# Routers, their norms and the expert tables moved on behind every second piece of other work; gates from a hyperbolic tangent

## The chip, the cores and the metric

The kernel runs on one core of one Trainium2 chip. The metric is the device time of one execution in microseconds (us). A core has five engines with a queue of instructions each, which run in order: TensorE (PE in the profile, its weight loads PEld), VectorE (DVE), ScalarE (ACT), GpSimd (POOL) and SyncE (SP). SP, ACT and POOL also issue DMA transfers. An instruction that waits for a semaphore holds up what stands behind it on its engine.

## What is computed

Sixty-four sequences of 64 tokens with 128 features pass four layers; a second tensor of the same shape is the context. Layer 0 is attention with relative positions and a feed-forward part. Layer 1 is self-attention, cross-attention and a feed-forward part. Layer 2 gates pooled context into the tokens. Layer 3 is self-attention, cross-attention and a mixture of eight experts, of which each token takes two. The change touches that mixture:

```python
h = _ln(x, ln_g, ln_b)
logits = h @ rw.T + rb
vals, idx = jax.lax.top_k(logits, K)          # K = 2
gates = jax.nn.softmax(vals, axis=-1)
...
h1 = jax.nn.gelu(jnp.einsum('nd,efd->enf', hf, fc1_w) + fc1_b[:, None, :], approximate=False)
eo = jnp.einsum('enf,edf->end', h1, fc2_w) + fc2_b[:, None, :]
...
mixed = (gathered * gates_f[..., None]).sum(axis=1).reshape(x.shape)
return x + mixed
```

Of two logits a >= b the softmax gives 1/(1+e) and e/(1+e) with e = exp(b - a), which is the same as 0.5 + 0.5 tanh((a - b)/2) and 0.5 - 0.5 tanh((a - b)/2).

## The kernel before

The 4096 tokens are cut into eight groups (g = 0 to 7) of 512 tokens, four blocks of 128. Layer 0 runs first, in an order written out by hand. Everything after it is written as Python generators, which issue a piece of their instructions and then yield. A driver, `drive` (line 149), decides whose piece is issued next. Outside layer 0 the order in which instructions are issued here is a priority: a scheduler in the language lays each engine's final order, and may put an instruction ahead of earlier ones when it takes it to be ready.

The driver goes round in rounds. In each it may start one attention task (self-attention or cross-attention of one group) and one light task (feed-forward of layer 1, or layer 2). Attentions are started four rounds apart, three once no light task is left. Then each running task issues one piece, in the order of their start. Then the driver takes a step of the `fill` generator, which is `experts` (line 669): one step a round, and two or three by turns once the flag `done["exponentials"]` is set. When all tasks have ended, the rest of `fill` is issued at once.

`cross3` (line 1292) is the last attention of a group. It has 15 pieces before its closing one, which adds the result to `x`. Then, still in the same generator, come the norm (`normalise`, line 281, into the tile `zx`, four buffers), the transposes, and `router` (line 1320): the logits `lg`, the two best experts by comparisons (`cand`, `hot`), the difference `e2` and its exponential (called `e` in the profile), the rank of each token in its expert by two matmuls (`pr`), the gates, and eight scatters of rows, `hrows<-zx,to`, indirect DMAs that POOL issues. The column of `zx` that holds the token number is written by a copy from `tok`, which depends on nothing but the buffer. At the end the router counts up `done["routed"]`. In the last group three of the router's yields are left out.

The eight groups are in two parts, five and three (`PARTS`). `experts` waits until five groups are routed, makes the first table (`table`, line 677: which expert's rows lie in which slot of 128 rows), waits for the exponentials flag, which the last group's cross-attention sets when it issues its last softmax exponentials, and goes through 47 slots of the first part and 31 of the second. In each slot: a load of 128 rows on SP (`km<-hrows`, which waits until all scatters of its part have landed), a transpose (`xt`), an activation on ACT (`vp`), four matmuls with the first expert matrix and four with the second (all named `f`; the profile counts each twice, so sixteen per slot), Gelu on ACT, an addition on DVE, and a scatter on POOL (`yrows<-km,tob`). The second part's table waits until all eight groups are routed. At the end the rows are read back, weighted by the gates (`summed`, line 820), and written out.

Of the kernel before, what the change touches and what calls it, by code (L numbers as in the profile page):

```python
# [12 lines left out]
AF = mybir.ActivationFunctionType  # L13
ALU = mybir.AluOpType
AX = mybir.AxisListType

P = 128
# [5 lines left out]
NBLK = T // P  # L23
# [10 lines left out]
ROWW = D + 2  # L34
# [60 lines left out]
def kernel(ctx: ExitStack, tc: tile.TileContext, a: dict, out: bass.AP):  # L95
    order = {"on": False}
    nc = Ordered(tc, order)
# [14 lines left out]
    def wtile(shape, tag, bufs, dtype=F32):  # L112
        if tag in COMMON:
            return pools["common"].tile(shape, dtype, tag=tag, bufs=COMMON[tag], name=tag)
        return pools["work"].tile(shape, dtype, tag=tag, bufs=bufs, name=tag)
# [29 lines left out]
    def mid(ap, n):  # L145

        return ap.unsqueeze(1).to_broadcast([ap.shape[0], n, ap.shape[1]])

    def drive(phases, lags, ends, fill):

        todo = {kind: [] for kind in lags}
        for n, (start, kind) in enumerate(phases):
            for g in range(NG):
                todo[kind].append((n, g, start))

        todo["light"].sort(key=lambda task: task[1])
        passed = {(-1, g) for g in range(NG)} - {(-1, g) for g, gen in ends}
        count = 0
        running, wait = [(-1, g, gen) for g, gen in ends], {kind: 0 for kind in lags}
        while running or any(todo.values()):
            for kind, tasks in todo.items():
                if wait[kind] <= 0:
                    for task in tasks:
                        n, g, start = task
                        if (n - 1, g) in passed:  # L170
                            tasks.remove(task)
                            running.append((n, g, start(g)))
                            wait[kind] = lags[kind] - (kind == "attention" and not todo["light"])
                            break
                wait[kind] -= 1
            for task in list(running):
                n, g, gen = task
                if next(gen, "end") == "end":
                    running.remove(task)
                    passed.add((n, g))  # L180
            count += 1
            for _ in range(2 + count % 2 if done["exponentials"] else 1):
                next(fill, "end")
        for _ in fill:
            pass

# [482 lines left out]
    def experts():  # L669
# [7 lines left out]
        def table(h):  # L677

            cnt = wtile([P, NE], "cnt", 1)
            nc.vector.tensor_tensor(cnt, endbase[h], start, ALU.subtract)  # L680
            cmp = v3(wtile([P, 512], "pT", 7)[:, 0 : NE * (REGION - 1)], NE)
            nc.vector.tensor_tensor(
                cmp, last(cnt[:, :], REGION - 1), mid(limit[:, :], NE), ALU.is_gt
            )
            nb = wtile([P, NE], "nb", 1)
            nc.vector.tensor_reduce(nb, cmp, axis=AX.X, op=ALU.add)
            cum = wtile([P, NE], "cum", 1)
            nc.vector.tensor_copy(cum[:, 0:1], nb[:, 0:1])
            for e in range(1, NE):
                nc.vector.tensor_tensor(cum[:, e : e + 1], cum[:, e - 1 : e], nb[:, e : e + 1], ALU.add)  # L690
            yield
            ns = NSLOT[h]
            counts = wtile([P, 512], "pT", 7)
            past = v3(counts[:, 0 : ns * NE], ns)
            jb, rb = (counts[:, (NE + k) * ns : (NE + k + 1) * ns] for k in range(2))
            nc.vector.tensor_tensor(past, last(index[:, 0:ns], NE), mid(cum[:, :], ns), ALU.is_ge)
            eb = wtile([P, ns], f"eb{h}", 1)
            nc.vector.tensor_reduce(eb, past, axis=AX.X, op=ALU.add)
            nc.vector.tensor_tensor(past, past, mid(nb[:, :], ns), ALU.mult)
            nc.vector.tensor_reduce(jb, past, axis=AX.X, op=ALU.add)  # L700
            yield
            nc.vector.tensor_tensor(jb, index[:, 0:ns], jb, ALU.subtract)
            nc.vector.scalar_tensor_tensor(rb, eb, float(REGION), jb, op0=ALU.mult, op1=ALU.add)

            nc.vector.tensor_scalar(rb, rb, float(NE * REGION), float(P), ALU.min, ALU.mult)
            tab = wtile([1, 2, ns], f"table{h}", 1, I32)
            nc.vector.tensor_copy(tab[:, 0, :], rb[0:1, :])
            nc.vector.tensor_scalar(
                tab[:, 1, :], eb[0:1, :], float(NE - 1), float(D), ALU.min, ALU.mult
            )  # L710

            hot = wtile([NE, ns], "hotb", 1)
            nc.vector.tensor_scalar(hot, eb[0:NE, :], lane[0:NE, :], None, ALU.is_equal)
            yield
            pb = extra("pb")
            for c in range(NFC):
                nc.tensor.matmul(
                    pb[:, c * ns : (c + 1) * ns], lhsT=fc1bT[:, c, :], rhs=hot, start=True, stop=True
                )
            hb = v3(wtile([P, NBLK * S], "mb", 3)[:, 0 : NFC * ns], NFC) if h == 0 else v3(room[:, used : used + NFC * ns], NFC)  # L720
            nc.vector.tensor_copy(hb, v3(pb[:, 0 : NFC * ns], NFC))
            tables[h] = tab, eb, hb
# [109 lines left out]

        while done["routed"] < PARTS[0]:
            yield
        yield from table(0)
        while not done["exponentials"]:
            yield

# [8 lines left out]
        for t in range(-6, total + 2):  # L847
            h = sum(t + 6 >= at for at in LAST)
            while h < NH and done["routed"] < sum(PARTS[: h + 1]):
                yield  # L850
            if h < NH and h not in tables:
                yield from table(h)
            if 0 <= t < total:
                first(t)
            if 0 <= t - 2 < total:
                second(t - 2)
            if t + 6 < total:
                load(t + 6)
            if 0 <= t + 1 < total:
                stage_weights(t + 1)  # L860
            if 0 <= t + 2 < total:
                turn(t + 2)

            for h in range(NH - 1):
                gl, at = divmod(t - 2 - LAST[h] - 4, 4)
                if 0 <= gl < PARTS[h]:
                    g = sum(PARTS[:h]) + gl
                    if at == 0:
                        reads[g] = read(g)
                    if at == 2:  # L870
                        summed(g, reads.pop(g))
            yield
# [8 lines left out]
    def other_layers(ends):  # L881
# [410 lines left out]
        def cross3(g):  # L1292
            x = xs[g]
            ct = ctx_of(g, 3)
            pc = transpose4(ct.rearrange("p b i -> p (b i)"))
            cz = wtile([P, T], "z", 4)
            nc.scalar.copy(cz, pc)
            yield
            kvT, qT = yield from together(
                ln_turned(cz, "ckv_g", "ckv_b", cz), ln_turned(x, "cq_g", "cq_b")  # L1300
            )
            add_row(x, obias[:, 1, :])
            yield
            ps = yield from attention(
                qT[:, :], v3(kvT[:, :], NB), in3[:, 1, 0:D], in3[:, 1, D : 2 * D], in3[:, 1, 2 * D :],
                wo3[:, 1, :], sc3, bias=1, then=(lambda: done.update(exponentials=True)) if g == NG - 1 else None,
            )
            nc.vector.tensor_tensor(x, ps, x, ALU.add)
            yield

            zx = wtile([P, NBLK, ROWW], "zx", 4)
            yield from normalise(zx.rearrange("p k c -> p (k c)"), x, width=ROWW)
            yield
            pt = transpose4(zx.rearrange("p k c -> p (k c)"), ROWW)
            hT = wtile([P, T], "T", 4)
            nc.scalar.activation(hT, pt, AF.Identity, scale=col("moe_g"), bias=col("moe_b"))
            yield
            yield from router(g, hT, x, zx)

        def router(g, hT, x, zx):  # L1320

# [7 lines left out]
            tops, hots = [], []  # L1329
# [22 lines left out]
            both = wtile([P, NBLK, NE], "both", 3)  # L1352
            nc.vector.tensor_tensor(both, hots[0], hots[1], ALU.add)
            e2 = wtile([P, NBLK], "e2", 3)
            g1 = wtile([P, NBLK], "g1", 3)
            nc.vector.tensor_tensor(e2, tops[1], tops[0], ALU.subtract)
            nc.scalar.activation(e2, e2, AF.Exp)
            yield

            pr = extra("pr")  # L1360
# [5 lines left out]
            for k in range(NBLK):  # L1366
                if k + 1 < NBLK:
                    dst = before[:, k + 1, :]
                else:
                    h, gl = PLACE[g]  # L1370
# [4 lines left out]
                )  # L1375
            nc.vector.tensor_tensor(before, before, v3(pr[:, 0 : NBLK * NE], NBLK), ALU.add)
            yield
            nc.vector.tensor_scalar(g1, e2, 1.0, None, ALU.add)
            nc.vector.reciprocal(g1, g1)
            nc.vector.tensor_copy(gate[:, g, 0, :], g1)  # L1380
            nc.vector.tensor_tensor(gate[:, g, 1, :], e2, g1, ALU.mult)

            def meta(c):
                return zx[:, :, D + c : D + c + 1].rearrange("p k c -> p (k c)")
# [48 lines left out]
    gate = mtile([P, NG, 2, NBLK], "gate")  # L1433
# [92 lines left out]
```

## Time and profile before

| what | value |
|---|---|
| three runs | 1685.83, 1694.06, 1694.51 us; median 1694.06 |
| the profiled execution | 1692.51 us, of it 1690.5 us from the first to the last instruction (the span) |
| busy share of the span | PE 92%, PEld 68%, DVE 69%, ACT 59%, POOL 53% |
| mean granted clock of PE | 0.943 |
| scatters of rows, `hrows<-zx,to` | 64, from 1415.8 to 1542.0 us |
| scatters of results, `yrows<-km,tob` | 78, mean 991 ns |
| ACT table loads | 2, mean 1283 ns |

Times of single instructions are counted from the start of the span. Almost all instructions carry line L74, the helper that records them, so they are told apart by engine, operation and tile: `a<-b,c` is an instruction that writes tile a and reads b and c. "Busy tenths" cut the span in 40 slices of 42.3 us, a digit being the busy share of an engine in tenths; PEclk is the share of full speed that was granted to TensorE's clock.

### The profile page before, as it was taken

To read this page: it belongs to the slowest core of one execution; us is meant where nothing else is said; L and a number is where in the kernel's file an instruction comes from. 1 tells how busy PE (TensorE), PEld (TensorE's weight loads), DVE (VectorE), ACT (ScalarE), POOL (GpSimd) and SP (SyncE) were. 2 spreads that over 40 slices of the span, in tenths; PEclk is the share of its full clock that TensorE was granted. 3 is DMA by queue.
4 is the path that set the end of the run, shared out by engine and by line. 5 is a ranking of instruction groups with operands and counts; after the bars stand their busy time and mean duration, and the time that the engine had idled before them with its cause. 6 is when DMAs were issued, how large, how long until landed. Compare 5 with 4: busy or idle time off the path is not lost. (4 is left out here: it accounts for less than half of the span.)

```text
span 1690.5 us, 45408 instructions
## 1 busy us (share of the span) xinstructions
PE 1548.2 (92%) x17588; PEld 1155.6 (68%) x17588; DVE 1161.5 (69%) x3147; ACT 1002.6 (59%) x2744; POOL 903.5 (53%) x867
## 2 busy tenths in 40 slices
PE   7799999999999999978888999989988998859995
PEld 4466666667666666646766776666767776759995
DVE  4477686777777677758887787677766677555554
ACT  4456556555555555535775655466767786427774
POOL 2445455555556464657886766653422234467543
PEclk9899999999999999979999999889998998759998
DMA  6756554555555555541000100000000000013243
GB/s 165 156 145 147 133 146 121 139 133 134 131 147 133 130 138 143 140 143 28 12 18 27 27 20 20 8 14 2 2 8 14 15 2 27 25 55 88 68 124 109
DMA packets 218356, 136.74 MB, mean 81 GB/s; under 512 B 38904, under 2 KB 202882, under 8 KB 218016
## 3 DMA queue, kind: packets, MB, share of 16 engines
q1 hardware_dynamic: 187024, 90.99, 23.1%
q10 hardware_dynamic: 26576, 34.40, 6.2%
q0 software_dynamic: 4544, 8.47, 1.6%
q8 instruction: 140, 2.29, 0.6%
q14 instruction: 72, 0.59, 0.1%
HBM read 66.95 MB, written 67.78 MB: 80 GB/s over the span
## 5 line engine op out<-in xcount | busy, mean ns | idle before, releaser
L74 ACT ACTIVATE s<-s,nm 128x128 f32<-128x128 f32 x512 | 198.1, 388 | 249.1 <-DVE nm L74 225.8
L74 POOL TENSOR_TENSOR s<-s,sm 128x512 f32<-128x512 f32 x128 | 130.4, 1039 | 251.8 <-DVE sm L74 251.8
L74 PE MATMUL pt<-ident,s 128*128 128x128 f32 x1536 | 216.3, 285 | 26.0 <-ACT kT L74 10.6
L74 POOL TENSOR_TENSOR s<-s,mx 128x512 f32<-128x512 f32 x160 | 164.3, 1046 | 99.1 <-DVE mx L74 92.9
L74 PEld LDWEIGHTS pt<-ident,s 128*128 128x128 f32 x1536 | 179.9, 146 | 46.4 <-issue 17.7
L74 ACT ACTIVATE pT<-pt 128x512 f32<-128x512 f32 x256 | 141.0, 601 | 78.1 <-PE pt L74 69.6
L74 POOL TENSOR_TENSOR skew<-skew,mb 128x512 f32<-128x512 f32 x128 | 159.9, 1271 | 40.3 <-DMA skew<-scr 39.6
L74 POOL TENSOR_TENSOR rs<-rs,nhalf 128x4 f32<-128x4 f32 x80 | 81.5, 1019 | 186.1 <-DVE rs L74 157.0
L74 PEld LDWEIGHTS av<-vb,pT 128*64 128x64 f32 x4096 | 134.1, 144 | 22.2 <-issue 13.2
L74 PE MATMUL av<-vb,pT 128*64 128x18 f32 x4096 | 142.3, 217 | 5.3 <-DVE o L74 4.8
L74 DVE TENSOR_REDUCE mx<-s 128x8 f32<-128x512 f32 x160 | 103.0, 677 | 44.4 <-ACT s L74 44.4
L74 PE MATMUL psk<-kv,wk 128*128 128x512 f32 x256 | 127.9, 622 | 0.0
L74 PE MATMUL psv<-wv,kv 128*128 128x256 f32 x512 | 127.4, 392 | 0.0
L74 PE MATMUL sc<-km,qs 32*64 32x256 f32 x2048 | 105.4, 422 | 9.4 <-ACT qs L74 5.4
L74 POOL DMA_INDIRECT yrows<-km,tob x78 | 77.3, 991 | 58.6 <-DVE tob L74 29.7
L74 DVE COPY pT<-pt 128x512 f32<-128x512 f32 x128 | 82.2, 683 | 37.3 <-PE pt L74 37.3
L74 PEld LDWEIGHTS pbd<-rT,qp 64*128 64x128 f32 x1024 | 63.0, 189 | 58.6 <-DVE qp L74 56.9
L74 PEld LDWEIGHTS psv<-wv,kv 128*128 128x128 f32 x512 | 92.2, 189 | 15.1 <-issue 1.0
L74 PEld LDWEIGHTS av<-pT,v 128*64 128x64 f32 x2048 | 66.5, 138 | 50.7 <-issue 29.0
L74 DVE TENSOR_TENSOR s<-sc,mb 128x512 f32<-128x512 f32 x128 | 82.5, 682 | 26.7 <-PE sc L74 26.7
L74 DVE TENSOR_TENSOR s<-psc,skew 128x512 f32<-128x512 f32 x128 | 87.5, 684 | 14.2 <-issue 6.3
L74 ACT ACTIVATION_READ_ACCUMULATOR s<-s,nm 128x1 f32 x512 | 95.6, 187 | 0.0
(231 smaller groups left out, 3564.0 us busy)
## 6 DMA issues: line engine op xcount, KB each, us to landing
scr<-stage SPq DMA_DIRECT2D x64, 516.0 KB
skew<-scr SPq DMA_DIRECT2D x128, 256.0 KB
hrows<-pad ACTq DMA_DIRECT2D x66, 325.0 KB
ctx<-in_ctxT SPq DMA_DIRECT2D x24, 256.0 KB
km<-hrows SPq DMA_DIRECT2D x78, 65.0 KB
fcw<-in_fc ACTq DMA_DIRECT2D x16, 256.0 KB
kv<-in_xT SPq DMA_DIRECT2D x8, 256.0 KB
kv<-in_ctxT SPq DMA_DIRECT2D x8, 256.0 KB
```

The source lines that it names most:

```text
L74: ins = it(*args, **kw)
```

## The change

The driver gets a second kind of task. A generator that yields the word `CHAIN` instead of nothing is noted as a chain, and from then on it isn't given one piece a round: it moves on after every second piece of the other tasks, once more at the end of the round, and after each step of the fill. The closing norm and the router of `cross3` become chains (with one yield more, after the tile `zx` is taken), and so does the making of a table in `experts`; while the fill is in a chain, its steps come with the chains. The gates are made from a hyperbolic tangent of half the difference of the two logits: the exponential, an addition, a reciprocal, a copy and a product become the tangent and two multiply-adds.

```diff
@@ -146,7 +146,14 @@
 
         return ap.unsqueeze(1).to_broadcast([ap.shape[0], n, ap.shape[1]])
 
+    CHAIN = "chain"
+
+    def chain(gen):
+        for _ in gen:
+            yield CHAIN
+
     def drive(phases, lags, ends, fill):
+
 
 
 
@@ -160,8 +167,25 @@
 
         todo["light"].sort(key=lambda task: task[1])
         passed = {(-1, g) for g in range(NG)} - {(-1, g) for g, gen in ends}
-        count = 0
+        count, chains, filling = 0, set(), [None]
         running, wait = [(-1, g, gen) for g, gen in ends], {kind: 0 for kind in lags}
+
+        def advance(task):
+            n, g, gen = task
+            said = next(gen, "end")
+            chains.discard(task)
+            if said == "end":
+                running.remove(task)
+                passed.add((n, g))
+            elif said == CHAIN:
+                chains.add(task)
+
+        def advance_chains():
+            for task in [task for task in running if task in chains]:
+                advance(task)
+            if filling[0] == CHAIN:
+                filling[0] = next(fill, "end")
+
         while running or any(todo.values()):
             for kind, tasks in todo.items():
                 if wait[kind] <= 0:
@@ -173,14 +197,19 @@
                             wait[kind] = lags[kind] - (kind == "attention" and not todo["light"])
                             break
                 wait[kind] -= 1
+            beats = 0
             for task in list(running):
-                n, g, gen = task
-                if next(gen, "end") == "end":
-                    running.remove(task)
-                    passed.add((n, g))
+                if task not in chains:
+                    advance(task)
+                    beats += 1
+                    if beats % 2 == 0:
+                        advance_chains()
+            advance_chains()
             count += 1
             for _ in range(2 + count % 2 if done["exponentials"] else 1):
-                next(fill, "end")
+                if filling[0] != CHAIN:
+                    filling[0] = next(fill, "end")
+                    advance_chains()
         for _ in fill:
             pass
 
@@ -832,7 +861,7 @@
 
         while done["routed"] < PARTS[0]:
             yield
-        yield from table(0)
+        yield from chain(table(0))
         while not done["exponentials"]:
             yield
 
@@ -849,7 +878,7 @@
             while h < NH and done["routed"] < sum(PARTS[: h + 1]):
                 yield
             if h < NH and h not in tables:
-                yield from table(h)
+                yield from chain(table(h))
             if 0 <= t < total:
                 first(t)
             if 0 <= t - 2 < total:
@@ -1309,13 +1338,14 @@
             yield
 
             zx = wtile([P, NBLK, ROWW], "zx", 4)
-            yield from normalise(zx.rearrange("p k c -> p (k c)"), x, width=ROWW)
-            yield
+            yield CHAIN
+            yield from chain(normalise(zx.rearrange("p k c -> p (k c)"), x, width=ROWW))
+            yield CHAIN
             pt = transpose4(zx.rearrange("p k c -> p (k c)"), ROWW)
             hT = wtile([P, T], "T", 4)
             nc.scalar.activation(hT, pt, AF.Identity, scale=col("moe_g"), bias=col("moe_b"))
-            yield
-            yield from router(g, hT, x, zx)
+            yield CHAIN
+            yield from chain(router(g, hT, x, zx))
 
         def router(g, hT, x, zx):
 
@@ -1352,9 +1382,8 @@
             both = wtile([P, NBLK, NE], "both", 3)
             nc.vector.tensor_tensor(both, hots[0], hots[1], ALU.add)
             e2 = wtile([P, NBLK], "e2", 3)
-            g1 = wtile([P, NBLK], "g1", 3)
-            nc.vector.tensor_tensor(e2, tops[1], tops[0], ALU.subtract)
-            nc.scalar.activation(e2, e2, AF.Exp)
+            nc.vector.tensor_tensor(e2, tops[0], tops[1], ALU.subtract)
+            nc.scalar.activation(e2, e2, AF.Tanh, scale=0.5)
             yield
 
             pr = extra("pr")
@@ -1375,10 +1404,9 @@
                 )
             nc.vector.tensor_tensor(before, before, v3(pr[:, 0 : NBLK * NE], NBLK), ALU.add)
             yield
-            nc.vector.tensor_scalar(g1, e2, 1.0, None, ALU.add)
-            nc.vector.reciprocal(g1, g1)
-            nc.vector.tensor_copy(gate[:, g, 0, :], g1)
-            nc.vector.tensor_tensor(gate[:, g, 1, :], e2, g1, ALU.mult)
+
+            nc.vector.tensor_scalar(gate[:, g, 0, :], e2, 0.5, 0.5, ALU.mult, ALU.add)
+            nc.vector.tensor_scalar(gate[:, g, 1, :], e2, -0.5, 0.5, ALU.mult, ALU.add)
 
             def meta(c):
                 return zx[:, :, D + c : D + c + 1].rearrange("p k c -> p (k c)")
```

## The prediction

> **What bounds it now.** First I read the busy tenths by slices: TensorE (PE) holds 9 in most slices and breaks once, to 8-8-5 in slices 34 to 36, some 1440 to 1520 us. That break is what I cost. I then cut the stretch into windows (start:end, us, then busy us of PE, PEld, DVE, ACT, POOL, granted clock, DMA share, GB/s):
>
> ```profile
> PE   7799999999999999978888999989988998859995
> PEclk9899999999999999979999999889998998759998
> ...
> 1400.00:1420.00 20.00, 19.29 (x271) 14.41 (x271) 16.99 (x77) 15.37 (x32) 7.78 (x8) 0.85 0.02 5
> 1450.00:1460.00 10.00, 4.94 (x42) 4.45 (x26) 5.75 (x25) 1.46 (x3) 2.56 (x3) 0.74 0.05 16
> 1490.00:1500.00 10.00, 1.83 (x9) 1.70 (x8) 2.23 (x19) 0.00 (x0) 7.82 (x9) 0.50 0.17 54
> 1500.00:1510.00 10.00, 6.13 (x24) 5.01 (x24) 7.26 (x55) 2.52 (x6) 7.68 (x8) 0.50 0.14 47
> 1560.00:1600.00 40.00, 40.00 (x358) 39.79 (x357) 20.68 (x93) 31.59 (x105) 21.51 (x22) 1.00 0.27 72
> ```
>
> PE is the limit up to 1420 and again from 1545, where the experts run. Between, it idles and its granted clock is 0.50, while POOL is the busiest engine. Weighting PE's busy time by the clock in ten-us windows leaves about 42 us of full-rate work in the 86 us from 1430 to 1516: some 44 us are to be had at most.
>
> The tile view of `zx` says what POOL does there, and the timelines of DVE and ACT who waits (start, duration; in brackets the idle time before and its releaser):
>
> ```profile
> L74 POOL DMA_INDIRECT hrows<-zx,to x64: 954/958/1274, 1415.8 to 1542.0; - x64
> L74 ACT ACTIVATE zx<-x,nmr,rs x32: 478/483/540, 1353.7 to 1501.4; 128x128 f32<-128x128 f32 x32
> ```
>
> ```profile
> 1430.23 0.17 DVE L74 COPY zx<-tok 128x4 f32<-128x4 f32 x1 [6.05 <-DMA hrows<-zx,to]
> ...
> 1453.27 0.17 DVE L74 COPY zx<-tok 128x4 f32<-128x4 f32 x1 [5.07 <-DMA hrows<-zx,to]
> ...
> 1500.02 0.16 DVE L74 SCALAR_TENSOR_TENSOR nmr<-mv,rs 128x4 f32<-128x4 f32 x1 [6.97 <-POOL rs L74]
> ```
>
> ```profile
> 1477.64 0.60 ACT L74 ACTIVATE pT<-pt 128x512 f32<-128x512 f32 x1 [0.26 <-PE pt L74]
> ...
> 1500.21 1.65 ACT L74 ACTIVATE zx<-x,nmr,rs 128x128 f32<-128x128 f32 x4 [11.94 <-DMA hrows<-zx,to]
> ...
> 1516.81 1.28 ACT L74 ACT_TABLE_LOAD   x1
> ```
>
> The first router's norm runs at 1353.7, its first scatter at 1415.8. All 64 row scatters come after that, each 0.96 us and 0.30 us to the next, 1.27 in all: 81 us of POOL, nearly back to back from 1486 to 1542. With four `zx` buffers, groups 4 and 5 wait for the scatters of groups 0 and 1, and group 7's norm 11.94 us for those of group 3. The experts need 40 of the scatters. The chain of waits shows them released by one of these, the load being followed by the first expert matmuls:
>
> ```profile
> 1510.36 2.27 DMA hrows<-zx,to
> ...
> 1513.87 1.91 DMA km<-hrows
> 1515.82 0.48 PE xt L74
> 1516.30 1.71 PE f L74 x8
> ```
>
> The last attention exponential had ended at 1478.2. So 38 us lie between it and the first expert, and they belong to late routers.
>
> **Why the routers are late.** From norm to logits, logits to `e`, and `e` to first scatter, group 0 takes 20 us each (1353.7, 1373.7, 1394.2, 1415.8): that is one start interval of cross3, three rounds of the driver. A router with norm has 12 pieces after its first and gets one a round. That is the order of issue, not data: group 7's norm-to-logits, with nothing else running, takes 5 us (1500.2 to 1505.2).
>
> **The change, part by part.** (1) *Driver.* Stepping through both loops piece by piece: with five other tasks running, chains advance after the second, the fourth, at the round's end and after the fill's step, four times a round. Group 0's router is issued in 3 rounds instead of 13; group 4's is done in round 123, table 0 in round 125, the round that issues the last attention exponentials. Before, these were rounds 132 and 133. The experts then start with that exponential. Nothing is added or removed; moved are, per router, some 30 small DVE operations of 0.15 to 0.19 us (about 5 us), 20 matmuls (`tr` 0.64, `pl` 1.06, `pr` 0.8: 2.5 us of PE at full clock), one ACT pass and 8 scatters (10.2 us of POOL).
>
> (2) *Where the scatters land.* Into the attention stretch, where POOL is busy about 6.4 us in 20 (`rs` three times 1.02, `s` twice 1.04, `x` 1.3). With 10.2 it is at 16.6 of 20: it fits, in bursts. What queues behind a burst on POOL is `rs` and `s`; DVE's `nmr` stands behind `rs`, and all DVE work behind `nmr`. Cost per burst: below, 0.9, the ordinary wait of `nmr` (no extra); above, the 6.97 of 1500.02, which came behind ten scatters. In the trace the two bursts that did run in the stretch (1415 to 1428, 1441 to 1452) brought no such wait, so I take no extra here and keep 6.97 for the range. On SP, the first expert load waits for the 40 scatters at the queue's head, and only later expert loads and the final transfers stand behind it: the last context load of an attention is issued with group 7's cross3 in round 113, ahead of it. 0.
>
> (3) *The zx copies.* The copy of the token numbers depends on the buffer alone and was placed on DVE before the scatters of four groups earlier had landed: 6.05 and 5.07 us on DVE, with 3.51 and 5.06 us of PE idle (its matmuls at 1433.16 and 1455.75). With early routers these two are gone (PE -8.6), but the same placement can recur behind each of the first four bursts: 0 to 4 times 4.3. Nearest are the two seen, one per burst; but the bursts now end long before the norms need the buffer, so I take two, +8.6.
>
> (4) *Router work moved forward.* The intervals grew 20.0, 20.6, 21.6 as routers joined; all are now like the last: +1.6 +1.0 = +2.6.
>
> (5) *Gates.* Out go `g<-e` 300 ns, reciprocal 170, copy 186, product 165; in come two operations like `zx<-ci` at 178: DVE -0.47 us a router, -3.7 in all. Only the final sums read the gates: 0 on the path, and 3.7 of DVE at most if that cover were gone.
>
> (6) *Tanh for Exp.* Same shape; `e<-e` took 209 ns, and on 128x512 Tanh took 630 against Exp 601: 0. The table is the open point. The trace has two table loads in all, one at the start and one before the first Gelu, so Tanh (used in the second layer) shares a set with Exp. Whether it shares Gelu's no row shows. Routers 6 and 7 now fall among Gelus: 0 to 4 loads of 1.28, 0 to 5.1 us. I take 0, since before every non-Gelu function among the experts (Identity on `vp`) needed no load; Exp kept there would run the same risk.
>
> The Trainium skill speaks against this part: "ScalarE: Activation LUTs", section "Table sets: the hidden batching unit", lists tanh with exp and with sigmoid and not with gelu, and asks to finish one set before the next; with its 2.66 us per switch, four switches would be an estimated 10.6 us. No run here shows which holds.
>
> **The sum**, on the profiled execution (span 1690.5, 1692.5 with its surroundings, so +2.0; 1.5 under the median 1694.06 of runs from 1685.83 to 1694.51). Last attention exponential 1478.2 - 8.6 + 8.6 + 2.6 = 1480.8, and there the first expert matmul. 78 slots of 1.90 (sixteen `f` 1.79, one `xt` 0.11, as the chain repeats them) = 148.2. PE work that now runs beside them: the last attention's end, some 3.5, and three routers, 7.5: 11. A start among scatters: before, PE waited 2.15 at 1541.4 and ran 1.85 slower after it: 4. From the last expert matmul to the end, as now, 1672.6 to 1690.5: 17.9. Together 1661.9, with 2.0 1663.9; +1.5 to the median: **1665 us**, 1.7% faster.
>
> **Rivals.** *The full gain.* No copy waits at all and no start among scatters: 1665 - 8.6 - 4 = 1652. For it: routers are two groups ahead of their buffers. Against: POOL serves 1.27 per expert slot and the last scatters still mix in.
> *POOL takes the place of the routers (the slower side).* Every burst from group 0 to group 6 falls on live attention and costs DVE the 6.97 us: 1665 + 7 x 6.97 = 1714. It outweighs the gain from (1694 - 1665) / 6.97 = 4.2 bursts. For it: POOL at 16.6 of 20, in order, with PE at 19.3 of 20 and nothing to catch up with. Against: the two bursts seen, though few `rs` fell near them.
> *The order of issue isn't what decides.* Instructions outside the first layer are reordered by a scheduler, as the copy at 733 us, long ahead of its router, shows; if the routers ran late for other reasons the time stays at 1694. Against: lags of exactly one interval per three pieces.
> *Tables.* Four loads: 1665 + 5.1 = 1670, the same side.
>
> **Numbers.** Chances: forecast, tables included, 0.47; full gain 0.23; POOL 0.20; no effect 0.10. About 0.5% (8.5 us) is what a measurement can tell from no change; the first two lie under 1685.6, so faster 0.70, same 0.10, slower 0.20. The range begins below the full gain by the four router periods' 2.6 and a further 8 for slots that slip in before the last exponential, 1641, and ends at 1700, with five bursts at full price. The forecast's own: none to four copy waits, with tables, 1656 to 1679.
>
> **What would show it.** Right: first scatter near 1375, the 40th by 1470; first `f` within 5 us of the last attention exponential; no slice under 8 before the end; ACT_TABLE_LOAD x2. Wrong: DVE waits for `rs` or for `hrows` of over 4 us in each interval after 1360 (step 2 or 3), loads beyond two (step 6), scatters still after 1415 (step 1).

## The result, and the profile after

The changed kernel takes 1707.28 us (median of four runs, 1705.94 to 1709.66) beside 1689.94 us of the kernel before in the same series (four runs, 1683.79 to 1694.51). The ratio is 1.010, 95% interval 1.008 to 1.012: **1% slower**, where 1.7% faster was forecast. 1707 lies above the range, which ended at 1700, and nearest to the rival in which POOL takes the place of the routers (1714).

The page of the changed kernel, in busy tenths, and the windows in the same stretches as before (us; busy us of PE, PEld, DVE, ACT, POOL; granted clock; DMA share; GB/s):

```profile
PE   7799999999999999969898999899989877878995
...
PEclk9899999999999999979999999889998978779998
```

```profile
1400.00:1420.00 20.00, 14.91 (x232) 11.36 (x218) 12.03 (x40) 12.83 (x25) 10.58 (x11) 0.93 0.07 25
1450.00:1460.00 10.00, 4.47 (x37) 3.54 (x38) 1.12 (x4) 2.43 (x5) 3.25 (x4) 0.50 0.06 20
1490.00:1500.00 10.00, 7.99 (x112) 6.91 (x112) 7.00 (x32) 5.75 (x12) 4.31 (x5) 0.96 0.06 16
1500.00:1510.00 10.00, 5.47 (x92) 5.24 (x92) 7.20 (x45) 2.53 (x6) 5.04 (x7) 0.89 0.13 40
```

The one break of 8-8-5 has become a long shallow one. From 1400 to 1420 us PE was busy 19.29 of 20 us before and is busy 14.91 now: the stretch that was full has holes. In 1450 to 1460 no engine is busy for even half the time: everybody waits. The tile view of `zx` and the timelines of POOL, DVE, ACT and PE (start, duration, in brackets the idle time before and its releaser) say for what:

```profile
L74 POOL DMA_INDIRECT hrows<-zx,to x64: 954/958/1232, 1377.2 to 1569.4; - x64
L74 ACT ACTIVATE zx<-x,nmr,rs x32: 477/482/495, 1352.1 to 1544.7; 128x128 f32<-128x128 f32 x32
```

```profile
1387.23 0.96 POOL L74 DMA_INDIRECT hrows<-zx,to  x1 [0.30 <-issue]
1388.22 1.05 POOL L74 TENSOR_TENSOR rs<-rs,nhalf 128x4 f32<-128x4 f32 x1
...
1389.31 0.16 DVE L74 SCALAR_TENSOR_TENSOR nmr<-mv,rs 128x4 f32<-128x4 f32 x1 [7.16 <-POOL rs L74]
...
1389.51 1.65 ACT L74 ACTIVATE zx<-x,nmr,rs 128x128 f32<-128x128 f32 x4 [6.74 <-DVE nmr L74]
...
1390.05 0.48 PE L74 MATMUL tr<-ident,zx 128*128 128x128 f32 x1 [6.62 <-ACT zx L74]
...
1421.61 0.16 DVE L74 SCALAR_TENSOR_TENSOR nmr<-mv,rs 128x4 f32<-128x4 f32 x1 [6.96 <-POOL rs L74]
...
1453.92 0.16 DVE L74 SCALAR_TENSOR_TENSOR nmr<-mv,rs 128x4 f32<-128x4 f32 x1 [6.96 <-POOL rs L74]
```

The first scatter comes at 1377.2 and not 1415.8 us, so routers did move forward. But the burst of group g ends exactly where the closing norm of group g+1 asks for its `rs`: on POOL `rs` starts 0.03 us after the last of eight scatters, DVE has by then waited 7.16 us, ACT 6.74 and PE 6.62. It happens to groups 1, 2 and 3 in the same way. In the next three norms DVE waits about 1 us for `rs`, and 4.82 in the last one (1543.3), when the experts already run.

At the other end, PE around the start of the experts, DVE's table, and ACT:

```profile
1508.93 0.23 DVE L74 TENSOR_SCALAR hotb<-eb,lane 8x47 f32<-8x47 f32 x1
...
1509.31 1.91 PE L74 MATMUL pb<-hotb,fc1bT 8*128 8x47 f32 x8 [4.53 <-DVE hotb L74]
1513.06 0.64 PE L74 MATMUL pr<-both,tri 128*128 128x32 f32 x2 [1.85 <-DVE mb L74]
...
1516.54 3.60 PE L74 MATMUL av<-vb,pT 128*64 128x18 f32 x64 [2.41 <-DVE before L74]
1520.07 0.48 PE L74 MATMUL xt<-ident,km 128*128 128x128 f32 x1
...
1522.27 1.87 PE L74 MATMUL pl<-rw,T 128*128 128x8 f32 x8 [0.66 <-ACT T L74]
1524.00 1.09 PE L74 MATMUL tr<-ident,o 128*128 128x128 f32 x4
1524.88 1.92 PE L74 MATMUL f<-vp,h 128*128 128x128 f32 x8
...
1525.72 1.28 ACT L74 ACT_TABLE_LOAD   x1
...
1531.62 0.19 ACT L74 ACTIVATE e<-e 128x4 f32<-128x4 f32 x1
```

The last attention exponential starts at 1507.1. Around and after it PE waits 4.53 + 1.85 + 2.41 = 8.8 us for the table (`hotb`, `mb`) and for a router (`before`), while the last attention's own products `av` stand behind them in its queue; the experts' first `xt` stands behind `av`, and the first `f` comes 17.7 us after the exponential. The tangent at 1531.62 lies between Gelus, and no table load follows it: two loads in all, as before.

Where the 15.5 us of span went (1690.5 before, 1706.0 after): first norm to last attention exponential, both by their starts, 124.0 -> 155.1 (+31.1); from there to the first `f` 38.5 -> 17.7 (-20.7, from unrounded times); from there to the end 174.4 -> 181.1 (+6.7); the stretch ahead -1.6.

### The profile page after: what moved, and what is told of

The parts are those of the page before. It is cut to its first block, busy times and chain, and to the rows that moved or that the text cites. A ratio compares the mean times of both kernels' runs of the same rounds, so it can differ in the third digit from the quotient of the medians.

```text
span 1706.0 us, 45367 instructions
## 1 busy us (share of the span) xinstructions
PE 1545.1 (91%) x17588; PEld 1154.5 (68%) x17588; DVE 1156.0 (68%) x3131; ACT 1002.6 (59%) x2744; POOL 903.2 (53%) x867
## 5 line engine op out<-in xcount | busy, mean ns | idle before, releaser
L74 PEld LDWEIGHTS av<-vb,pT 128*64 128x64 f32 x4096 | 138.2, 147 | 34.6 <-issue 18.0
L74 PE MATMUL av<-vb,pT 128*64 128x18 f32 x4096 | 146.7, 218 | 14.2 <-DVE o L74 9.1
L74 PEld LDWEIGHTS av<-pT,v 128*64 128x64 f32 x2048 | 66.5, 138 | 50.8 <-issue 29.1
L74 DVE TENSOR_TENSOR s<-sc,mb 128x512 f32<-128x512 f32 x128 | 82.4, 680 | 26.3 <-PE sc L74 26.3
```

Source lines behind the costliest of these rows:

```text
L74: ins = it(*args, **kw)
```

## The experiments

Theory **P**: the bursts of scatters hold up `rs` on POOL, and behind it DVE, ACT and PE. Rival **C**: four steps a round put a serial chain of small operations too close together, and the engines, which run in order, stand still at every link. Later, for the gap between the last exponential and the first `f`: **T**, the table's pieces on DVE and its products on PE hold up the end of the last attention, and **R**, the table's work tiles wait for buffers that the attentions use.

Kernels sent together ran on one chip with the kernel before, and ratios are to it. The kernels e5 to e8, and e17 and e18, ran in two sets in which the kernel before itself took 1726.6 us and engines waited in a way that no other set shows (the last section); their times stand only against the kernels of their own set. The table has the other sets.

| kernel | us | ratio [95%] | intervals of the zx norms, groups 0 to 4 | first norm to last exponential | to first `f` |
|---|---|---|---|---|---|
| before | 1689.9 | 1 | 20.0 20.6 21.6 25.1 | 124.0 | 38.5 |
| changed | 1707.3 | 1.010 [1.008, 1.012] | 37.4 32.3 32.3 19.3 | 155.1 | 17.7 |
| e1 rs by reciprocal on DVE | 1675.2 | 0.993 [0.991, 0.994] | 26.9 23.8 23.6 19.0 | 128.3 | 16.5 |
| e2 scatters one a step | 1685.4 | 0.998 [0.997, 1.000] | 30.7 27.5 27.2 18.5 | 135.3 | 21.8 |
| e3 before, tangent alone | 1684.2 | 0.998 [0.997, 0.999] | 20.0 20.6 21.0 26.3 | 124.7 | 34.5 |
| e4 before, copy tied | 1673.0 | 0.992 [0.990, 0.993] | 20.0 20.6 21.6 20.7 | 112.0 | 37.0 |
| e9 changed, again | 1711.1 | 1.011 [1.008, 1.014] | 37.5 32.3 32.4 19.2 | 156.8 | 17.7 |
| e10 rs by Newton on DVE | 1687.5 | 0.998 [0.997, 1.000] | 30.4 25.9 25.6 23.8 | 136.5 | 17.3 |
| e11 two steps a round | 1700.0 | 1.005 [1.003, 1.007] | 23.6 34.3 28.0 24.8 | 146.9 | 17.1 |
| e12 e10, other PSUM | 1695.9 | 1.002 [1.000, 1.004] | 30.1 29.1 26.9 25.0 | 146.0 | 17.4 |
| e13 e10, table in one piece | 1694.9 | 1.002 [1.000, 1.004] | 30.5 25.9 25.6 23.8 | 140.5 | 17.4 |
| e14 e10, two steps a round | 1688.8 | 0.998 [0.996, 1.000] | 23.6 26.5 26.3 23.1 | 136.7 | 19.6 |
| e15 late chains | 1697.9 | 1.003 [1.001, 1.005] | 21.1 23.6 45.1 20.2 | 147.2 | 16.6 |
| e16 e15 with Newton, table in one piece | 1683.9 | 0.995 [0.994, 0.997] | 20.8 22.8 34.7 23.7 | 136.4 | 17.7 |

### e1 and e2: rs away from the bursts, or the bursts cut up

e1, in `normalise` (it leaves out the square root, so it tells where the time goes and isn't a kernel to be had):

```diff
-        nc.gpsimd.tensor_tensor(rs, rs, nhalf, ALU.pow)
+        if width != D:
+            nc.vector.reciprocal(rs, rs)
+        else:
+            nc.gpsimd.tensor_tensor(rs, rs, nhalf, ALU.pow)
```

> The changed kernel, with DVE making the factor rs in the norm ahead of the router as a plain reciprocal of the variance, where POOL raised it to the power -0.5; so this norm divides by the variance instead of its root, and all other norms are left on POOL. Theory P (the bursts of eight scatters on POOL hold up rs, and behind it nmr on DVE, zx on ACT and the transposes on PE, some 6.6 us a burst beyond the usual wait, in four to six of the bursts): the 5 to 7 us waits of nmr for rs in the zx norms are gone, the intervals between zx norms fall from 32-37 to 22-30 us, time 1668 to 1685. Theory C (the finer steps put a serial chain of small operations between the others' pieces, and the engines, which run in order, stand still at each link; POOL only comes with it): the intervals stay at 30 us or more and the time at 1698 or above.

e2, in `router`, after each scatter:

```diff
+                    if g < NG - 1 and 2 * k + 1 + n < 2 * NBLK:
+                        yield
```

> The changed kernel with one scatter per step of the chain instead of eight in one step (groups 0 to 6). Theory P: what stands behind a burst on POOL is now at most one or two scatters late, so no wait of nmr for rs in the stretch is over 2.6 us, and the time is 1675 to 1695. Theory C: waits for rs shorten, but the intervals stay at 30 us or more and the time is 1700 or above.

e1: 1675.2 us, 32 us under the changed kernel (1707.3). DVE's waits from 1350 to 1500 us (total us, times, longest), first of the changed kernel, then of e1:

```profile
DVE nmr L74 <- POOL rs L74: 26.9, 9, 7.2
```

```profile
DVE rec L74 <- PE av L74: 19.1, 8, 5.1
...
DVE nmr L74 <- POOL rs L74: 2.1, 3, 0.8
```

And e1's timeline at a norm that falls on a burst:

```profile
1399.72 1.04 POOL L74 DMA_INDIRECT hrows<-zx,to  x1 [0.32 <-DVE mv L74]
1401.07 0.96 POOL L74 DMA_INDIRECT hrows<-zx,to  x1 [0.30 <-issue]
...
1399.96 0.18 DVE L74 RECIPROCAL rs<-rs 128x4 f32<-128x4 f32 x1
1400.17 0.16 DVE L74 SCALAR_TENSOR_TENSOR nmr<-mv,rs 128x4 f32<-128x4 f32 x1
```

The burst is still there; `nmr` follows `rs` in 0.21 us beside it. Nothing else was edited, and the stretch up to the last exponential shrinks by 26.7 us: P, not C, for this part. (What is left is still 16.3 us longer than in e4, below.) The three intervals shrink by 10.5, 8.5 and 8.7 us, 9.2 a burst: the 7 us that is read off the wait, and 2.2 more that the wait doesn't show. e2 gets there in part (longest wait for `rs` 3.6 us in place of 7.2, total 11.8; expected was 2.6 at most), 22 us under the changed kernel and within its expectation.

### e3 and e4: the parts alone, in the kernel before

e3 takes the gates of the change into the kernel before. e4 changes one instruction there:

```diff
-            nc.vector.tensor_copy(meta(0), tok[:, PLACE[g][1] * NBLK : (PLACE[g][1] + 1) * NBLK])
+            nc.vector.scalar_tensor_tensor(
+                meta(0), ci, 0.0, tok[:, PLACE[g][1] * NBLK : (PLACE[g][1] + 1) * NBLK],
+                op0=ALU.mult, op1=ALU.add,
+            )
```

> The kernel before with the gates from the hyperbolic tangent alone, driver untouched. Both theories: no effect beyond 0.3% (1685 to 1695), two table loads, since the tangent was followed by Gelu without a load in the changed kernel. If the tangent did cost table loads here, three or more loads and up to 5 us more.

> The kernel before, with the copy of the token numbers into zx made to depend on the router's own indices (their number times zero is added), so that it can't be laid ahead of its router. By step 3 of the prediction the two waits of DVE for hrows (6.05 and 5.07 us, 4.3 us of PE each) go, and the time falls by 8.6 us, to about 1681 to 1683; the wait of 11.94 us of group 7's zx stays. Rival: these waits only fill time in which the routers are late anyway, and the time stays within 3 us of before.

e3: 3.9 us less (0.23% of 1688.4; by the interval 1.9 to 5.7). In its profile the part between last exponential and first `f` is 4.0 shorter (38.5 -> 34.5), the stretch ahead 0.7 longer, the end 1.1 shorter; two table loads. e4: 15.5 us less, nearly twice the 8.6 expected. The windows of e4 and of the kernel before from 1420 to 1440 us:

```profile
1420.00:1440.00 20.00, 20.00 (x301) 16.47 (x300) 16.76 (x65) 13.07 (x25) 10.92 (x11) 0.91 0.17 51
```

```profile
1420.00:1440.00 20.00, 16.46 (x207) 12.72 (x205) 13.65 (x53) 11.16 (x19) 7.98 (x9) 0.90 0.15 52
```

With the copy tied to its router, PE has no idle time there, and the stretch falls by 11.9 us, more than the two waits of DVE that went (6.05 + 5.07 = 11.1). **e4 is faster than both kernels**, by one instruction, with the driver untouched.

e4 also says what early routers cost when no copy waits for scatters and no wait for `rs` in the stretch is over 1.2 us. Both hold for e1 as for e4, and the two ran beside each other; its stretch is 128.3 us against 112.0. Of the 16.3 us between them PE idles 11.2 (14.9 against 3.7) and is busy 5.1 longer, for the same attentions. No run takes these 16 us apart.

### e5 to e12: the same with all of the computation, half the rate, other PSUM buffers

Dividing by the variance, e1 may send tokens to other experts. e5 and e10 make the true factor on DVE:

```diff
-        nc.gpsimd.tensor_tensor(rs, rs, nhalf, ALU.pow)
+        if width != D:
+            var = rs
+            rs, sq = wtile([P, NBLK], "rt", 3), wtile([P, NBLK], "sq", 3)
+            nc.vector.tensor_scalar(
+                rs.bitcast(I32), var.bitcast(I32), -0.5, 1597463007.0, ALU.mult, ALU.add
+            )
+            for _ in range(3):
+                nc.vector.scalar_tensor_tensor(sq, rs, -0.5, rs, op0=ALU.mult, op1=ALU.mult)
+                nc.vector.tensor_tensor(sq, sq, var, ALU.mult)
+                nc.vector.scalar_tensor_tensor(rs, sq, 1.5, rs, op0=ALU.add, op1=ALU.mult)
+        else:
+            nc.gpsimd.tensor_tensor(rs, rs, nhalf, ALU.pow)
```

> The changed kernel with the factor rs of the norm ahead of the router made on DVE, by three steps of Newton from a first guess taken from the bits of the variance (eleven small DVE operations; all that the reference wants is computed). If e1 gained because rs no longer stands behind the scatters on POOL: 1672 to 1684, with intervals between zx norms of 23 to 28 us. If e1 gained because dividing by the variance sent tokens to other experts: near the changed kernel, 1700 or above.

> The changed kernel in which chains move on twice a round (at its end and after the fill's step) instead of four times; bursts of eight scatters as they are, rs on POOL. Theory P: the bursts still meet rs in most intervals, so waits of nmr for rs of 4 to 7 us stay, and the time is 1695 to 1710. Theory C (links of a serial chain too close together): the intervals fall to 22 to 27 us and the time to 1675 to 1690. Against both: the router takes 6 to 7 rounds instead of 3, so the experts may start up to 10 us later after the last attention exponential.

> The kernel of e5, with the router's rank products pr and the table's products pb in the seven rotating PSUM buffers instead of the single one that they share with the attention's products av. Theory T (pr and pb, which stand ahead of the last av and wait for DVE's table work, delay the end of the last attention): from the last attention exponential to the first expert f 8 to 12 us instead of about 17, time 5 to 9 us under e5. Rival: pb still stands ahead of av in PE's order and waits for hotb, so no more than 2 us.

> The kernel before (driver untouched) with everything else that has helped or may: the copy that can't be laid ahead (e4), tangent gates (e3), rs of the router's norm by Newton on DVE (e5), pr and pb in the rotating buffers. If the gains add up: 1688 - 15.5 - 4 = 1668, less up to 6 for rs: 1662 to 1670. If early routers are worth something beyond that, e7 is under it; if the late routers are as good once nothing waits for POOL, e8 is not slower than e7.

e6 is the changed kernel with the `beats` advance in the round left out:

```diff
-                    if beats % 2 == 0:
-                        advance_chains()
```

e7 and e12 are e5 with `pr = pmm("pr")` and `pb = pmm("pb")` for `extra(...)`; e8 is the kernel before with e4's, e3's, e5's and e7's edits. These four ran where the kernel before took 1726.55 us: e5 1747.2 (ratio 1.012), e6 1746.5 (1.012), e7 1738.6 (1.008), e8 1722.4 (0.998). By its expectation e5 spoke against P; but its trace has waits that no run before had, for nothing that the profile names, and in this set the changed kernel itself wasn't run. So nothing is concluded from the four, and e5, e6 and e7 were run again (e10, e11, e12) beside the changed kernel (e9):

> The changed kernel itself, beside e10 to e12 on one chip. On the chip of e5 to e8 (where the kernel before took 1726 us and PE and ACT waited 17 to 30 and 35 to 65 us for their own instructions from 1350 us on) nothing says how slow it would be; on one like that of e1 to e4, 1705 to 1709. The three others are read against this run.

> The kernel of e5 again. If rs behind the scatters is what the change lost (theory P): 24 to 34 us under e9, as e1 was. If e1 gained only by sending tokens elsewhere, and e5's ratio of 1.012 is the truth: within 5 us of e9.

> The kernel of e6 again: chains on twice a round, bursts and rs as in the changed kernel. In e6 the waits of nmr for rs were no longer than 1.2 us: the bursts happened to fall between the rs. Theory P then gives 1675 to 1690 where the instruction waits of e6 are gone, and 1695 or more only if waits for rs of 4 us and more are back. Theory C gives 1675 to 1690 as well, so it is told from P by the waits for rs: 4 us and more in three intervals or more, and yet under 1690, is C.

> The kernel of e7 again: pr and pb in the rotating PSUM buffers. In e7 it was 8.6 us under e5; theory T: again 5 to 9 us under e10, with 8 to 14 us from the last attention exponential to the first f. Rival: under 2 us.

The changed kernel took 1711.1 us there, e10 1687.5: 23.6 us less, just short of what P expected (24 to 34) and far from the 5 at most of the rival. So e1's gain is mainly the place of `rs`, not other tokens. The stretch is 136.5 us against e1's 128.3; the ten more operations on DVE are the likely reason (it is busy 99.8 us there against 90.0), but e1 ran in another set. e11, with bursts whole and half the rate, is 11 us under e9; waits for `rs` of 3.8 to 6.3 us are back in four norms, two over and two just under the 4 us that P named, and the time, 1700, is what it expects of them. e12 misses: 8.4 us **over** e10, where e7 was 8.6 under e5; the gap is 17.4 in place of 8 to 12. Beside e10, other PSUM buffers for `pr` and `pb` don't start the experts earlier.

### e13 to e18: what else is lost

e13 is e10 with the yields inside `table` taken out; e14 is e10 with e6's edit; e15 gives routers one piece a round while attentions are still to be started, and ties the copy as e4 does:

```diff
-                if task not in chains:
+                if task not in chains or todo["attention"]:
                     advance(task)
                     beats += 1
-                    if beats % 2 == 0:
+                    if beats % 2 == 0 and not todo["attention"]:
                         advance_chains()
-            advance_chains()
+            if not todo["attention"]:
+                advance_chains()
...
```

> The kernel of e10 (changed kernel, rs of the router's norm on DVE) with each table issued in one piece instead of four. Theory T (the table's pieces stand on DVE between others that wait for PE): the first km load within 10 us of the table's first operation (23 in e10), the first f 5 to 10 us after the last attention exponential (17 in e10), 6 to 12 us under e10's ratio of 0.998, so a ratio of 0.991 to 0.995. Rival: the start of the experts is set by the last attention's own tail, and the ratio stays at 0.996 to 1.000.

> The kernel of e10 with chains moved on twice a round instead of four times. Theory C (links too close together): intervals between zx norms of 21 to 24 us (24 to 28 in e10), the last attention exponential 10 us or more earlier, the ratio to before 0.990 to 0.995. Against C: intervals as in e10, and the ratio 0.996 or more.

> The changed kernel in which routers and tables get one piece a round, as before, as long as an attention is still to be started, and go on as chains only after that; the copy of the token numbers as in e4; rs on POOL. In the stretch up to some 1430 us it is e4. If early routers help only the tail: first expert 5 to 15 us earlier than in e4 against the last exponential (37 us there), ratio 0.983 to 0.990 (e4: 0.9916). If bursts hold up rs in the tail as well: 0.990 to 1.000.

> The kernel of e15 with rs of the router's norm on DVE and each table in one piece. If rs behind the bursts and the table's pieces are the two costs of going early: under e15 by 3 to 10 us, ratio 0.978 to 0.988. If not: the same as e15 within 3 us.

None of the four reached the ratio hoped for, and e13 (1.002) and e15 (1.003) lie beyond what even their rivals expected. e14: half the rate, and the same ratio and stretch as e10 (0.998; 136.7 and 136.5 us): the rate of the chains decides nothing once `rs` is off POOL, so C, as a matter of the rate, falls here too. e13: gap 17.4, as in e10. Its table's first operation still came 14 us after `cnt` on DVE. e15: the third interval is 45.1 us, and DVE's timeline has the longest wait for `rs` of all runs in it:

```profile
1441.48 1.23 DVE L74 SCALAR_TENSOR_TENSOR nmr<-mv,rs 128x4 f32<-128x4 f32 x1 [9.46 <-POOL rs L74]
```

Routers turned into chains together, and their bursts stand one behind another on POOL: DVE had the variance ready at 1425.5, and POOL raised it to the power at 1440.4, after twelve scatters, the first of them already running. e16, without that wait, is 14 us under e15 (more than the 3 to 10 expected; ratio 0.995), but still 34.7 us in that interval and 17.7 in the gap, and by its ratio not better than e4.

In e13's trace the table's work tiles come from the ring of seven `pT` buffers that the attentions use. e17 is e10 with two buffers for them alone:

```diff
-            cmp = v3(wtile([P, 512], "pT", 7)[:, 0 : NE * (REGION - 1)], NE)
+            cmp = v3(wtile([P, NE * (REGION - 1)], "cmp", 1), NE)
...
-            counts = wtile([P, 512], "pT", 7)
+            counts = wtile([P, 512], "counts", 1)
```

e18 is the kernel before with the edits of e3, e4, e5 and e17.

> The kernel of e10 (changed kernel, rs of the router's norm on DVE) with two buffers of its own for the table's work tiles, which were taken from the ring of pT buffers of the attentions. Theory R (the ring): the table's operation after cnt follows it within 2 us (13 in e10), pb no longer waits for hotb ahead of the last av, the first f comes 6 to 11 us after the last attention exponential (17 in e10), ratio 0.990 to 0.995 (e10: 0.998). Rival: something else binds the start of the experts, gap 15 us or more, ratio 0.996 to 1.000.

> The kernel before, driver untouched, with the copy that can't be laid ahead (e4), gates by the tangent (e3), rs of the router's norm on DVE and the table's own buffers. Gains of e4 (0.9916) and e3 (0.9977) together, and group 7's wait for rs (7.25 us in e4) and the table's late end off the chain: ratio 0.980 to 0.990. Rival: the Newton steps lie in DVE's queue among the attentions and cost what they save, 0.990 to 0.996.

Both ran where the kernel before took 1726.67 us: 1743.7 (ratio 1.011) and 1722.3 (0.997), and both miss the ratios hoped for. The ring did bind the table's start: its operation after `cnt` follows by 0.24 us where it took 12.7 in e10. That the ring sets the gap isn't shown: it is 17.9 us, not the 6 to 11 of theory R, and though e5 had 24.4 in a set of the same kind, e6 and e7 had 17.8 and 18.7 there with the ring as it was. What e17's buffers would be worth where the kernel before takes 1690 us, and whether e18 beats e4 there, stays open.

## Why the prediction was wrong, step by step

By its own terms the sum gave a span of 1661.9; measured is 1706.0. It counts from the end of the last attention exponential, 0.6 us after its start. So counted, the 44.1 between them are: the start 1.6 earlier; first norm to the end of the last exponential 155.7 in place of 1480.8 - 1353.7 = 127.1, so 28.6 more; 17.1 from there to the first `f` in place of 0; and from the first `f` to the end 181.1, where the terms 148.2 + 11 + 4 + 17.9 come to 181.1 as well.

- **Step (2), where the scatters land, failed, and it cost most.** "I take no extra here": e1, which frees `rs` alone, gives back 26.7 of the 28.6 us. The evidence for no extra was the two bursts seen before; they began right behind a norm's `rs` (1415.8, 1441.0, the starts of `zx`), so none stood behind them. Busy time (16.6 of 20) says that POOL has room, and nothing of where in the interval the burst falls. With four steps a round a router takes about one interval, so the bursts of groups 0, 1 and 2 each ended up ahead of the next group's norm. The rival had the mechanism and the place; its price was seven bursts at 6.97 us, 48.8 in all, against three at 9.2. That its 1714 lies so near to 1707 is in part luck: the late start of the experts, which it didn't have, makes up most of the rest.
- **Step (1), the driver, half right.** The first scatter moved (1377.2, forecast near 1375), but the 40th, for which the experts wait, came at 1505.4 and not by 1470: 1.2 us earlier than before (1506.6), because the stretch had grown (in e1 it came at 1475.2). It is now ahead of the last exponential, not 28 us behind it. Yet "the experts then start with that exponential" failed: 17.1 us, and nearly as much in e1. Routing was no longer the last to come; the table's end (DVE, 1513.1) and the last attention's `av` behind `pb` and `pr` were. The prediction took the order of issue for the order of execution. Which share each has isn't settled: in one piece (e13) or with other PSUM buffers (e12) the gap stays at 17.4; buffers of its own (e17) free the table's start, but the gap stays at 17.9, and that in one of the sets at 1726.6 us.
- **Step (3), the copies, off in both directions.** After the change no wait of the copies for scatters is left (0.2 us in all), as in the rival of full gain, not two. And the two of before were worth more than 4.3 each: e4 gives 11.9 us in the stretch. PE's idle time right at the wait (8.6) was too low a price; DVE's whole wait (11.1) came nearer.
- **Step (4), router work moved forward, was sized too low.** 2.6 us were forecast; e1's stretch is 16.3 longer than e4's, with no copy and no `rs` behind scatters in either. So it is luck that e1's stretch, 128.9 us to the exponential's end, lies within 1.8 of the forecast's 127.1: copy waits that didn't come back (-11.9 in place of 0) hide what early routers cost (+16.3 in place of 2.6). With the 26.7 of step (2) the three make the 31.1 us by which the stretch grew. What the 16.3 consist of stays open.
- **Step (5), gates, taken as 0**: in the kernel before they are worth 3.9 us (e3), near the 3.7 named for the case that the cover is gone. That this is the reason isn't shown.
- **Step (6), the table**, right: two loads in every run, though in the changed kernel a tangent lies between Gelus. The trace doesn't bear out what was feared from the Trainium skill, "ScalarE: Activation LUTs", section "Table sets: the hidden batching unit", which lists tanh with exp and with sigmoid and not with gelu: an estimated 10.6 us for four switches; measured are 0.

The signs of error named beforehand were seen: DVE waits for `rs` of over 4 us in the first three intervals after the first burst (step 2), and scatters long after 1415 (step 1). Of the signs of being right only the first scatter and the two table loads came.

## What to carry to other kernels

Before work is moved onto an engine that has room, look at what small operation stands behind it there and who waits for that: where the two coincide the price goes by the burst (here 11 us long: 7.0 of waiting, 9.2 of time), whatever the busy share, and a regular schedule can make them coincide several times running (here three). An instruction that depends only on a buffer's release can be laid ahead of its turn and stall its whole engine; one false dependence was worth more here (e4, 0.8%) than the whole reordering, which lost 1%. When a sum comes out right, check its terms by runs that change one each: here two errors of over 11 us hid each other. An early start is bounded by the next late thing, so name it (here the table, and the products queued behind it) before the gain is booked in full.

## What the runs showed of the hardware

The same kernel before took 1688 to 1692 us (medians) in four of the six sets of runs and 1726.6 and 1726.7 in two. The number of the chip doesn't tell them apart: e5 to e8 and e13 to e16 are both on record with number 10, and the kernel before took 1726.6 us in the one set and 1691.9 in the other. In the two sets at 1726 us, and nowhere else, PE and ACT wait long for something that the profile doesn't name (`issue`: for nothing that it shows; `remote`: for a semaphore with no releaser in it); ACT's waits from 1350 to 1600 us in e5:

```profile
ACT pT L74 <- remote: 22.9, 4, 8.5
...
ACT vb L74 <- remote: 11.9, 3, 4.8
ACT vp L74 <- remote: 11.9, 3, 6.1
ACT s L74 <- remote: 10.7, 2, 6.1
```

On PE, ACT and DVE none of them comes between 800 and 1376 us in e5 and e8, and they begin after the first row scatter: the first over 1 us at 1383.7 in e5 (first scatter 1376.3), at 1420.4 in e8 (1409.2). On PE and ACT together they make 86 us in e5, 0.6 in the kernel before in its own profile. That instructions come late there, and that the scatters slow their loading, is a guess; no run takes it apart. The kernel of e10 has a ratio of 1.012 in such a set (e5) in place of 0.998.

Over a whole stretch, lost clock and idle time of PE go together. From the first norm to the last exponential PE idles 3.7 us in e4, 12.3 before, 14.9 in e1 and 37.8 in the changed kernel, and the mean granted clock is 0.89, 0.87, 0.85 and 0.80. From one window to the next they don't: in the changed kernel PE is busy 14.9 of the 20 us from 1400 at a clock of 0.93, and 15.7 of the next 20 at 0.68. Whether the clock makes the 2.2 us that a burst costs beyond its wait isn't shown.
